# A two-layer graph attention network in f32: the second layer's aggregates 1 to 4 split a second time

## The chip, the cores and the metric

The kernel runs on one core of one Trainium2 chip. The metric is the device time of one execution in microseconds (us). The engines are called PE (TensorE, the matrix unit; PEld is its loading of weights), DVE (VectorE), ACT (ScalarE), POOL (GpSimd) and SP (SyncE, which here only issues transfers).

## The reference, cut to what matters

N is 2708 nodes, all widths are 1024, everything is float32. Each layer normalises its rows, makes attention weights under the mask `adj`, and multiplies them by rows:

```python
h = jnp.maximum(_layernorm(x, axis=-1), 0.0)
# layer 0
f, g = h @ Wf + bf, h @ Wg + bg
attention = softmax(jnp.where(adj > 0, relu(f @ g.T), -9e15), axis=1)
x = x + attention @ (h @ W + bW)
# layer 1 (on the new x and its own h)
hw = h @ W
e = leaky_relu(hw @ a1 + (hw @ a2).T, 0.2)
attention = softmax(jnp.where(adj > 0, e, -9e15), axis=1)
x = x + relu(attention @ hw)
```

## The kernel before

**Order of products.** Attention times (h times W) is computed as (attention times h) times W. The first product is called the aggregate, the second the projection. Every big product is done by a form of Strassen's scheme with seven products of halves in place of eight, here named M1 to M7. Each needs sums of the operands' quarters, and sums of the results.

**Tiles.** The 2708 rows are twenty tiles of 128 rows, a tile MONO of 128 and a tile TINY of 20. The output is made in five panels `p`, of 576, 576, 532, 512 and 512 rows (`width`). The twenty tiles form ten pairs (`pairs`, NQ = 10); a panel owns two pairs, 2p and 2p + 1.

**Stages.** Layer 0 goes panel by panel: scores, the next panel's `project_q`, `aggregate(0, p)`, `project(0, p)`. As a panel's projection ends, its rows of x are complete; `rows_done` normalises them and `pair_h` forms, for a pair of tiles, the seven first-level combinations of rows and stores them in DRAM, in `hg_d[1]`, one tensor for two pairs, in rows of 512 elements. Layer 1 then runs, for each panel, `aggregate(1, p)` and `project(1, p)` (lines 1544 to 1550).

**An aggregate** (line 841). The left operand is a tile of row combinations from DRAM (`hc`, 128 x 2 x 512, loaded on SP), the right one is a weight tile `S[t]` (128 x width) or a first-level sum of weight tiles' halves. `accumulate` (line 603) walks through the products in the order M1, M5, M2, M6, M3, M7, M4; each is 10 pairs x 4 column groups `d`, a matmul of 128 x 128 by 128 x h with h half the panel's width (line 617), into four PSUM banks, one for each `d`. An evict function per product adds the bank to what is kept in SBUF. The sums of the weights are made on DVE: `T1` at the start, `second` after M5, `fourth` after M2 (10, 20 and 10 subtractions of 128 x h). `left_over` (line 877) adds MONO's and TINY's part. After M3, `inverse_sums` inverts the row sums of the weights; after M7, `scale` (line 931) multiplies the results by them on POOL.

**What orders the work.** Loads keep the order in which the program issues them. Other instructions are put in order for each engine by a planner at build time. Small steps of DVE and ACT work wait in a list, `later`. Each step has an estimated cost; `behind(us)` (line 198) adds credit after a group of matmuls and issues steps from the list while credit is left. A step's own loads are issued up to `ahead` steps earlier. `exps_until` forces the weights' steps when they are needed.

**The next panel's weights.** `take_shifts(p + 1)` (line 1536) empties the list and makes the row maxima; `take_weights(p + 1)` (line 1540) puts 24 steps at the front of the list, 22 of which load a mask and do two ACT and up to three DVE operations on a weight tile. In layer 1 they hang on the products M3 and M7, the fifth and sixth in order (line 1548).

**Buffers.** `slots` holds 54 buffers of 128 x 576 (weights, temporaries), `strm` 12 buffers of 128 x 1024 (everything loaded in a stream, `hc` too), `psum` 8 banks.

## Time and profile before

| | us |
|---|---|
| median of three runs | 3134.34 (3131.34 to 3138.29) |
| span of the profiled execution | 3135.8 |
| layer 1, aggregate 0 (2157.3 to 2309.2) | 151.9 |
| layer 1, aggregate 1 (2357.1 to 2507.4) | 150.3 |
| layer 1, aggregate 2 (2569.1 to 2707.6) | 138.5 |
| layer 1, aggregate 3 (2760.3 to 2893.8) | 133.5 |
| layer 1, aggregate 4 (2941.7 to 3073.9) | 132.2 |

The profiled execution's own run time is not given apart; its span, from the first instruction to the last, lies 1.5 us above the median of the runs. All stage times are read from the span's start. The mean granted clock of TensorE is 0.989. In a group of instructions the first number is busy time, then the mean length of one in ns, then the engine's idle time before them and what ended it. A single matmul's length includes the time until its last result is out, so lengths of neighbours overlap; the time between starts is what a stream of them costs.

### The profile page before, as it was taken

What the parts mean: (1) busy time and instruction counts of PE and PEld (TensorE: products, weight loads), DVE (VectorE), ACT (ScalarE), POOL (GpSimd) and SP (SyncE); (2) the same over time, 40 slices, a digit from 0 to 9 for tenths busy, and PEclk for the clock granted to TensorE, in tenths of its full rate; (3) what the DMA queues carried; (4) which work ended last, traced back from release to release, by engine and by line L of the source; (5) the groups of instructions that cost most, each with busy time, mean ns of one, the idle gap of its engine ahead of it and who ended that gap; (6) DMA issues with size and microseconds to landing.
All of it is one profiled execution on the core that took longest, in us unless ns stands there. A gap on an engine that the chain in (4) does not pass through costs nothing.

```text
span 3135.8 us, 36310 instructions
## 1 busy us (share of the span) xinstructions
PE 3053.1 (97%) x12694; PEld 2266.1 (72%) x12694; DVE 1835.6 (59%) x3767; ACT 450.3 (14%) x785; POOL 427.3 (14%) x654
## 2 busy tenths in 40 slices
PE   8998999899999999999999999998999999999998
PEld 4576777657877588886888885875757758678684
DVE  5766693776741686426973377758573571745612
ACT  3420020010200101101020002103131130311200
POOL 1421101310002110023000101021010020120202
PEclk9999999999999999999999999998999999999999
DMA  6989967988546796468955678597655565565655
GB/s 220 294 252 248 292 247 253 301 275 230 175 136 156 222 247 223 149 153 253 284 180 160 171 214 245 191 293 250 200 179 175 158 200 158 171 197 172 219 169 181
DMA packets 386278, 666.04 MB, mean 212 GB/s; under 512 B 171744, under 2 KB 212224, under 8 KB 386096
## 3 DMA queue, kind: packets, MB, share of 16 engines
q1 hardware_dynamic: 341936, 536.96, 56.9%
q0 software_dynamic: 44160, 126.76, 12.6%
q8 instruction: 101, 1.65, 0.2%
q14 instruction: 81, 0.66, 0.1%
HBM read 548.26 MB, written 115.30 MB: 212 GB/s over the span
## 4 chain that ended last, share of the span: by engine, by line
PE 81%; issue 6%; DVE 6%; DMA 5%; SPq 1%; POOL 1%; ACT 0%; POOLq 0%; DVEq 0%; ACTq 0%
PE gz L617 11%; PE gx L617 11%; PE gy L617 10%; PE sz L1140 6%; PE pz L1029 5%; PE gv L617 5%; PE sx L1140 4%; PE sy L1140 4%; PE px L1029 4%; PE py L1029 4%; PE M_ps L530 3%; PE qz L617 2%; PE qx L617 2%; PE qy L617 2%; DVE junk L45 1%
## 5 line engine op out<-in xcount | busy, mean ns | idle before, releaser
L1140 PE MATMUL sz<-B,As 128*128 128x288 f32 (+2 forms) x1200 | 295.9, 396 | 12.1 <-DVE st L45 7.9
L1140 PEld LDWEIGHTS sz<-B,As 128*128 128x128 f32 x1200 | 229.4, 192 | 63.1 <-DVE st L45 11.8
L933 POOL TENSOR_TENSOR gT<-gT,rr 128x2304 f32<-128x2304 f32 (+5 forms) x20 | 73.0, 3648 | 1081.4 <-DVE rr L45 979.3
L1140 PE MATMUL sx<-B,As 128*128 128x288 f32 (+2 forms) x800 | 201.5, 395 | 11.2 <-DMA As<-hs_d 9.1
L1140 PE MATMUL sy<-B,As 128*128 128x288 f32 (+2 forms) x800 | 199.3, 392 | 0.0
L617 PE MATMUL gz<-Sa,hc 128*128 128x288 f32 (+2 forms) x800 | 190.3, 399 | 5.9 <-DMA hc<-hg_d 5.9
L617 PE MATMUL gx<-P,hc 128*128 128x288 f32 (+2 forms) x800 | 187.0, 394 | 0.1
L617 PE MATMUL gz<-P,hc 128*128 128x288 f32 (+2 forms) x800 | 185.5, 392 | 0.0
L1140 PEld LDWEIGHTS sx<-B,As 128*128 128x128 f32 x800 | 152.5, 191 | 45.2 <-DMA As<-hs_d 10.1
L617 PE MATMUL gy<-T,hc 128*128 128x288 f32 (+2 forms) x800 | 184.2, 391 | 0.0
L617 PEld LDWEIGHTS gz<-Sa,hc 128*128 128x128 f32 x800 | 154.6, 194 | 40.0 <-DMA hc<-hg_d 6.4
L617 PEld LDWEIGHTS gx<-P,hc 128*128 128x128 f32 x800 | 152.4, 191 | 34.2 <-issue 3.7
L1140 PEld LDWEIGHTS sy<-B,As 128*128 128x128 f32 x800 | 152.3, 191 | 30.8
L617 PEld LDWEIGHTS gz<-P,hc 128*128 128x128 f32 x800 | 151.3, 190 | 31.6 <-issue 1.8
L617 PEld LDWEIGHTS gy<-T,hc 128*128 128x128 f32 x800 | 152.0, 190 | 30.5
L1029 PE MATMUL pz<-w,ps 128*128 128x512 f32 x320 | 142.1, 594 | 0.8 <-DVE pt L45 0.8
L1029 PE MATMUL py<-w,ps 128*128 128x512 f32 x320 | 141.9, 593 | 0.0
L1029 PE MATMUL px<-w,gT 128*128 128x512 f32 x320 | 141.0, 593 | 0.0
L143 POOL DMA_DIRECT2D out_dram<-x_res x180 | 89.2, 502 | 269.7 <-DVE x_res L45 264.5
L1029 PEld LDWEIGHTS pz<-w,ps 128*128 128x128 f32 x320 | 60.2, 190 | 77.1 <-issue 71.0
L1029 PEld LDWEIGHTS py<-w,ps 128*128 128x128 f32 x320 | 60.6, 190 | 75.5 <-issue 73.1
L530 PE MATMUL M_ps<-wgT,wfT 128*128 128x512 f32 x256 | 112.9, 597 | 1.6 <-ACT hsT L45 1.6
(319 smaller groups left out, 4894.9 us busy)
## 6 DMA issues: line engine op xcount, KB each, us to landing
hc<-hg_d SPq DMA_DIRECT2D x350, 512.0 KB, 3.7
As<-hs_d SPq DMA_DIRECT2D x150, 512.0 KB, 5.2
w<-wt_d SPq DMA_DIRECT2D x96, 512.0 KB, 4.9
w<-in_L_gnn_W_dram SPq DMA_DIRECT2D x72, 512.0 KB, 4.8
md<-md_d SPq DMA_DIRECT2D x56, 512.0 KB, 5.7
adj_i<-in_adj_dram SPq DMA_DIRECT2D x200, 128.0 KB, 5.2
hs_d<-hsT POOLq DMA_DIRECT2D x40, 512.0 KB, 7.2
As<-hs_d SPq DMA_DIRECT2D x50, 256.0 KB, 4.8
```

The source lines that it names most:

```text
L45: i = f(*a, **k)
L143: nc.gpsimd.dma_start(a, b)
L530: nc.tensor.matmul(ps, wfT[a][c // NH][:, c % NH, :], wgT[b][c], start=(c == 0), stop=(c == NC - 1))
L617: nc.tensor.matmul(ps[d], left(m, k, d), right(m, k), start=(start and k == 0), stop=(k == K - 1), skip_group_check=True)
L933: nc.gpsimd.tensor_tensor(of(e, s), of(e, s), by(s, k), OP.mult)
L1029: nc.tensor.matmul(ps, left[i][m][:, k, :], w_[k], start=(start and k == 0), stop=(k == NH - 1), skip_group_check=True)
L1140: nc.tensor.matmul(ps[:n, :h], lefts[q][:, i % 2, c, :n], B[m][c // 2][:, c % 2, :h], start=(start and c == 0), stop=(c == NH - 1), skip_g ...
```

## The change

Aggregates 1 to 4 of layer 1 apply the seven-product scheme a second time, inside each of the seven products. Aggregate 0 of layer 1 and all of layer 0 keep one level.

- **Rows.** `hg_d[1]` is replaced by one tensor `hr_d`, whose rows lie in halves of 256 elements, and a tensor `hs2_d` holds the four second-level combinations that aren't rows of `hr_d` themselves. `put_quarters` makes them: for each product and each two pairs, two fetches on POOL's queue, four DVE operations of 128 x 256, two stores. These 35 steps wait in a second list, `lazy`, from which `behind` issues only when `later` is empty and `spare` is set: in layer 0's aggregates 1 to 4 and in layer 1's aggregate 0. What is still open when a product needs it is forced by `quarters_until`.
- **Aggregate.** `aggregate_quartered` runs the seven outer products in the order M1, M5, M2, M6, M7, M3, M4. Each is seven inner products of 5 x 2 matmuls of 128 x 128 by 128 x (h/2), both column groups in one bank. The inner M4 of an outer product follows the first inner product of the next one. Their results are joined in SBUF (`V`) and added to the places in G by `into_place`. `quarters_of` makes the second-level sums of the weights, 20 subtractions for each outer product, in the middle of the outer product before. `scale` runs in the last outer product.
- **Loads.** Each inner product loads 128 x 4 x 256; the fifth of the five row groups comes from two tiles loaded once for each outer product. Aggregate 0 of layer 1 reads its rows from `hr_d` in pieces of 256.
- **Next weights.** `take_shifts` hangs on M2 and `take_weights` on M6, the third and fourth outer product, except in aggregate 0, which keeps M3 and M7. The first outer product's sums are made in the projection before, at M7.

The diff, cut to its core:

```diff
-    hg_d = [[dram.tile([P, 7, len(g), W], FP, name=f"hg{l}_d{i}") for i, g in enumerate(groups)] for l in range(2)]
+    hg_d = [dram.tile([P, 7, len(g), W], FP, name=f"hg_d{i}") for i, g in enumerate(groups)]
+    NK = NQ // 2
+    WH = W // 2
+    hr_d = dram.tile([P, 7, 2, 2, NK, WH], FP, name="hr_d")
+    hs2_d = dram.tile([P, 7, 4, NK, WH], FP, name="hs2_d")
...
+        while spare[0] and not later and lazy and credit[0] > 0:
+            credit[0] -= one(lazy)
...
+    def put_quarters(m, k):
+
+        two = []
+
+        def fetch():
+            if from_slots[0]:
+                two.extend(slot(f"hq{h}", (P, 2, WH)) for h in range(2))
+            else:
+                t = stream("hq", (P, 4, WH))
+                two.extend(t[:, 2 * h:2 * h + 2] for h in range(2))
+            for h in range(2):
+                nc.gpsimd.dma_start(two[h], hr_d[:, m, h, :, k])
+
+        def go():
+            a11, a12, a21, a22 = (two[h][:, i] for h in range(2) for i in range(2))
+            add(a22, a21, a22)
+            sub(a21, a11, a21)
+            sub(a11, a22, a11)
+            sub(a12, a12, a11)
+            for h in range(2):
+                store(hs2_d[:, m, 2 * h:2 * h + 2, k], two[h])
+            made_quarters[m] = made_quarters.get(m, 0) + 1
+        put(1.7, go, fetch, to=lazy)
...
+        def make(m):
+            for k in range(NK):
+                r11, r12, r21, r22 = (part_of(m, k, i) for i in ((0, 0), (0, 1), (1, 0), (1, 1)))
+                four = slot("quarter", (P, 4, WX // 4))
+                t = {n: four[:, i, :hb] for i, n in enumerate((M5, M6, M7, M4))}
+                sub(t[M5], r12, r11)
+                sub(t[M6], r22, t[M5])
+                sub(t[M7], r22, r12)
+                sub(t[M4], r21, t[M6])
+                sums[m, k] = t
...
+        def product(m, n, ps, start):
+            quarters_until(m)
+            if (m, 0) not in lasts:
+                for i, of in enumerate((hr_d[:, m, :, :, NK - 1].rearrange("p h f c -> p (h f) c"), hs2_d[:, m, :, NK - 1])):
+                    lasts[m, i] = stream("hl2", (P, 4, WH))
+                    load(lasts[m, i], of)
+            t = stream("hc2", (P, NK - 1, WH))
+            raw = n in (M1, M2, M4)
+            i = {M1: 0, M2: 1, M4: 3, M6: 0, M3: 1, M7: 2, M5: 3}[n]
+            load(t, hr_d[:, m, i // 2, i % 2, :NK - 1] if raw else hs2_d[:, m, i, :NK - 1])
+            last = lasts[m, int(not raw)][:, i]
+            for k in range(NK):
+                for d in range(2):
+                    lhs = t[:, k] if k < NK - 1 else last
+                    nc.tensor.matmul(ps[:, d], lhs[:, d * P:(d + 1) * P], inner_right(m, n, k),
+                                     start=(start and k == 0 and d == 0), stop=(k == NK - 1), skip_group_check=True)
+            behind(fine)
...
+        def into_place(m, V, r):
+            for e, s in place[m]:
+                o = quad(e, s)[:, 2 * r:2 * r + 2]
+                if m == M1:
+                    nc.scalar.copy(o, V[r])
+                elif m == M5:
+                    add(o, o, quad(0, lo)[:, 2 * r:2 * r + 2])
+                else:
+                    add(o, V[r], o)
...
+        before_next = {M1: lambda: make(M5), M5: with_second, M2: lambda: (of_right["fourth"](), make(M6)), M6: lambda: make(M7),
+                       M7: lambda: make(M3), M3: lambda: make(M4)}
...
+            X = bank2("gx")
+            product(m, M1, X, True)
+            nc.scalar.copy(c21, X)
+            if m == M1:
+                of_right["fifth"]()
+            if left_out:
+                left_out()
+            Z = bank2("gz")
+            product(m, M6, Z, True)
+            add(c12, Z, c21)
+            Y = bank2("gy")
+            product(m, M5, Y, True)
+            add(c22, Y, c21)
+            if m == M7:
+                corner()
+            if m in before_next:
+                before_next[m]()
+            product(m, M2, X, False)
+            if m not in more_of:
+                nc.scalar.copy(c11, X)
+            product(m, M7, Z, False)
+            add(c22, Z, c22)
+            product(m, M3, Y, False)
...
+            add(c12, Y, c12)
...
-            then = {M3: lambda p=p: take_shifts(p + 1), M7: lambda p=p: take_weights(p + 1)}
-        g = aggregate(1, p, S, sm, then, rate=4.0)
-        project(1, p, g, finish1(p), by_pair=(p == NP - 1), rate=1.7)
+            then = dict(zip((M2, M6) if p else (M3, M7), (lambda p=p: take_shifts(p + 1), lambda p=p: take_weights(p + 1))))
+        spare[0] = p == 0
+        g = aggregate_quartered(p, S, sm, next_right, then, fine=1.0) if p else aggregate(1, p, S, sm, then, rate=4.0)
+        hooks = {}
+        if p + 1 < NP:
+            next_right = quarters_of(p + 1, got["P"][0])
+            hooks = {M7: next_right["first"]}
+        project(1, p, g, finish1(p), hooks, by_pair=(p == NP - 1), rate=1.7)
```

## The prediction

> **What bounds the kernel now.** I read the page's busy times first, then the busy times by stage of the second layer (windows cut where TensorE goes from aggregates to projections), then the groups by shape, then the order in time.
>
> ```profile
> PE 3053.1 (97%) x12694; PEld 2266.1 (72%) x12694; DVE 1835.6 (59%) x3767; ACT 450.3 (14%) x785; POOL 427.3 (14%) x654
> ```
> ```profile
> 2357.10:2507.40 150.30, 150.30 (x645) 115.83 (x644) 63.74 (x123) 20.98 (x38) 11.60 (x10) 1.00 0.53 162
> 2507.40:2569.10 61.70, 61.70 (x146) 27.26 (x145) 40.81 (x62) 20.33 (x33) 14.12 (x29) 1.00 0.55 171
> ...
> 2760.30:2893.80 133.50, 133.50 (x642) 115.54 (x641) 57.43 (x118) 18.98 (x34) 10.81 (x10) 1.00 0.59 180
> 2893.80:2941.70 47.90, 47.90 (x113) 21.11 (x113) 38.10 (x59) 17.19 (x28) 11.85 (x24) 1.00 0.69 209
> 2941.70:3073.90 132.20, 132.20 (x630) 114.34 (x629) 34.59 (x80) 6.73 (x14) 10.79 (x10) 1.00 0.59 183
> ```
>
> These stages are, in order, panel 1's aggregate and projection, panel 3's two, and panel 4's aggregate. The columns are length, then PE, PEld, DVE, ACT, POOL, clock, DMA share, GB/s. PE is busy for every microsecond: the aggregates of layer two are TensorE time and nothing else. So time falls only if TensorE gets less to stream and is still fed.
>
> Next, how long a matmul takes. Each matmul of the source is two instructions (a product has 10 x 4 matmuls, and 80 stand in a row):
>
> ```profile
> 2357.23 19.40 PE gx L617 x80
> ```
> ```profile
> 2760.31 17.43 PE L617 MATMUL gx<-P,hc 128*128 128x256 f32 x80
> ```
> ```profile
> 61.64 1.04 PE L238 MATMUL sp_ps<-ident,v 128*128 128x128 f32 x8
> 62.52 1.91 PE L399 MATMUL h_ps<-ident,x 128*128 128x128 f32 x16
> ```
> ```profile
> 62.41 1.78 PEld L399 LDWEIGHTS h_ps<-ident,x 128*128 128x128 f32 x16
> 64.16 0.30 PEld L530 LDWEIGHTS M_ps<-wgT,wfT 128*128 128x128 f32 x2
> ```
>
> At 288 columns: 19.40 / 80 = 0.2425 us. At 256 columns: (17.43 - 0.38 for the last one's drain) / 79 = 0.2158. At 128 columns, with new weights each time, the 16 transposes take (1.91 - 0.27) / 15 = 0.1091. All three lie on one line, 0.834 ns per column and almost nothing fixed, so a matmul of half the width costs half.
>
> **What the Trainium skill says.** "TensorE: Matmul & The Clock Gate", LDWEIGHTS (loading the stationary operand): a load takes the number of columns over 1.2 GHz, 107 ns for 128. Groups by shape record an ordinary f32 load here as 190 ns, which would swamp a 128-column matmul. But the two ordinary loads in the row at 64.16 together last 0.30 = 0.11 + 0.19: the second started 0.11 after the first. So 190 is latency, the engine is held about 0.11 us, and the page fits. "VectorE: DVE Perf Modes", the errata section on SBUF-source operations: a fixed cost per instruction, whatever the size. It agrees: subtractions run 0.367 us apart at 288 elements and 0.335 at 256 (rows below), about 0.07 of it fixed. "GPSIMD Engine Reference", Specifications: its SBUF interfaces are shared with VectorE where a VectorE instruction has two SBUF inputs. It agrees, and strikingly:
>
> ```profile
> 2464.36 5.05 POOL L933 TENSOR_TENSOR gT<-gT,rr 128x2304 f32<-128x2304 f32 x1 [98.87 <-DVE rr L45]
> ```
> ```profile
> 2465.14 4.30 DVE L45 TENSOR_TENSOR z<-f,mcol 128x5 f32<-128x5 f32 x1
> ```
>
> A five-column operation lasted 4.30 us, until POOL's scaling ended. "DMA: Bandwidth & Descriptors", Specifications: line rate from 512 bytes on, so I cost the new 1 KB pieces of the sums' rows at their bytes; no row here isolates such a load.
>
> **The change part by part.** *Aggregates 1 to 4, matmuls.* Before: 7 x 10 x 4 x 2 = 560 instructions of h = 288, 266, 256, 256 columns. After: 49 x 5 x 2 x 2 = 980 of 144, 133, 128, 128. By the line: 560 x (0.2425, 0.2242, 0.2158, 0.2158) = 135.8, 125.6, 120.8, 120.8. After, 980 x (0.1224, 0.1133, 0.1091, 0.1091) = 120.0, 111.0, 106.9, 106.9. It saves 15.8 + 14.6 + 13.9 + 13.9 = **58.2 us**, all on the path. The left-over rows keep their work (16 instructions of h become 32 of h/2 over twice the banks, and the short ones go in groups of four as before): 0.
>
> *Second-level sums of the weights.* 7 x 5 x 4 = 140 subtractions of 128 x h/2 per panel on DVE.
>
> ```profile
> 2363.16 3.03 DVE L45 TENSOR_TENSOR T<-P 128x288 f32<-128x288 f32 x8
> ```
> ```profile
> 2764.51 3.10 DVE L45 TENSOR_TENSOR T<-P 128x256 f32<-128x256 f32 x9
> ```
>
> (3.03 - 0.45) / 7 = 0.367 and (3.10 - 0.42) / 8 = 0.335, hence about 0.216 at 144, 0.20 at 128: 30 us for panel 1, 28 for 3 and 4. *Evictions:* 38 + 4 of h elements for 28 before, 14 x 0.335 to 0.367 = 5. *Placing into G:* 16 of 2h elements, at twice 0.335 less the fixed 0.07, so 0.6 to 0.67: 10. The old 40 sums stay. So DVE gains 46 us in panel 1 and 42 in panel 3. The ledger of aggregate plus projection: panel 1, 63.7 + 40.8 + 46 = 150 of 212 - 16 = 196 us (77%); panel 3, 57.4 + 38.1 + 42 = 138 of 181 - 14 = 167 (82%); panel 4, which makes no next weights, near half. It fits, but no longer loosely. An inner product is now 20 instructions, 2.2 to 2.4 us, and a bank is wanted again two products later, so DVE may be late by some 4.4 us; a block of sums is 20 x 0.2 = 4, with a first-level block ahead of it 7 to 11. Behind such a block queue the evictions, and behind these TensorE. And the scaling's two POOL operations (5.1 + 2.6 us) now fall in the last outer product, beside the next weights' two-input additions, which they lock out. I put the waits at 4 us in panels 1 to 3 and 2 in panel 4: **+14**. Bounds: 0 (it all fits into the slack), and 4 x 29 = 115 (no sum is hidden).
>
> *Next weights earlier (third and fourth outer product).* The same instructions; 24 items at credit 2.1 against 21 inner products at 1.0 and the projection's 14 x 1.7, so about 10 in the aggregate, 11 in the projection, 3 in the next aggregate. The mask loads pass some aggregate loads on SP; these are fetched ahead. I cost the move at 0: the products M7, M3 and M4 and the projection hide it. If that cover is gone, every item that is late (three DVE operations, 2 us) stands ahead of the next aggregate's sums; with three left, 6 us a panel.
>
> *Loads of aggregates 1 to 4.* 35 of 512 KB become 49 + 14, +14.7 MB. Panel 3 moved 24.09 MB in its window, and the end of layer one shows what the engines can do:
>
> ```profile
> DMA packets 9782, 24.09 MB, mean 180 GB/s; under 512 B 1167, under 2 KB 3215, under 8 KB 9774
> ```
> ```profile
> DMA packets 9468, 24.23 MB, mean 362 GB/s; under 512 B 1076, under 2 KB 2612, under 8 KB 9465
> ```
>
> 38.8 MB in 133.5 - 14 = 119.5 us is 325 GB/s: below 362, with eight or nine tiles of 2.2 us fetched ahead. Taken as hidden; bounds 0 and, at the 301 GB/s of the busiest slice of the page, 129 - 119.5 = 9.5 us a panel.
>
> *Second-level sums of the rows.* 35 items of four DVE operations of 256 elements (1.34 us, 47 in all), two fetches and two stores each on POOL's queue, at 0.5 to 1.0 us an issue by POOL's groups. They lie in aggregates of layer one whose DVE is busy 36 to 39 us of 132 to 148 (82 of 132 in the last), and in aggregate 0 of layer two (106 of 152). POOL's queue waits there for fetched data; behind it stand mask stores and the scaling, none wanted within microseconds. Their 36.7 MB add 7.3 MB a stage. Only the end of layer one is open, where TensorE waits 8.3 and 3.9 us on a chain that began with mask loads 13.6 us long: **+4** for this, for the 1 KB pieces in aggregate 0 and for the split stores. Bounds: -1 (order shifts that chain either way) and 15.
>
> **Sum.** 58.2 - 14 - 4 = 40 us saved. The profiled span is 3135.8, 1.5 above the median of the runs, 3134.3, so it is a typical execution, and what lies around it doesn't change: 3134.3 - 40 = **3094**.
>
> **The rivals.** *Everything fits:* 3134 - 58 = 3076; the ledger of 77 to 82% speaks for it, the 4.4 us of tolerance against. *The transfers bind:* all four panels pay 9.5, and 3134 - 40 + 38 = 3132, no change; for it speaks 325 GB/s wanted, against it 362 held for 67 us. *The slower one: VectorE's blocks come between.* If each of the 28 outer products waits for its sums, the point from which it decides is 58.2 / 28 = 2.1 us each; at 2.8 us, two thirds of a block, they cost 78 us, and it ends at 3154. For it: first-level and second-level blocks stand together ahead of M2 and M6. Against: sums are issued half an outer product (7 to 9 us) early. *The weight load binds:* if 190 ns held the engine, 980 x 0.19 x 4 = 745 against 503 us before, 3376; the pair at 64.16 speaks against it. That the change doesn't do what it says I can't see: no condition but the panel's number chooses the split.
>
> **How the numbers follow.** Forecast (3076 to 3114) 0.60; everything fits 0.07; more is eaten but still faster (3114 to 3128) 0.08; transfers bind 0.08; VectorE's blocks 0.14; weight load 0.03. A measurement of this kernel tells 0.2%, 6 us, from no change, so faster is 0.75, the same 0.08, slower 0.17. The range 3074 to 3136 leaves out the last two and half of the second.
>
> **What would show it.** Right: narrow matmuls 0.109 to 0.123 us apart; aggregates of 135 to 139, 124 to 128, 120 to 124 and 118 to 120 us; DVE near 80% there; single TensorE gaps of 1 to 3 us released by DVE. Wrong: 0.19 spacing; gaps released by the row tiles' loads; gaps of over 2 us at every outer product; a longer stretch between the two layers.

## The result, and the profile after

| | before | after |
|---|---|---|
| median of four runs each, us | 3136.32 (3131.34 to 3140.34) | 3127.83 (3126.43 to 3136.15) |
| span of the profiled execution, us | 3135.8 | 3127.1 |

The ratio of the times is 0.9978, 95% interval 0.9958 to 0.9999. A repeat on another chip (21 runs of the changed kernel, 43 of the one before) gave 0.9989, 0.9982 to 0.9995. So by the two ratios the change saves 7 and 3 us where 40 were forecast; it lies at the edge of what a measurement tells from no change. Layer one and layer two are here what the code calls layers 0 and 1.

The page's busy times after the change:

```profile
PE 3016.9 (96%) x14630; PEld 2311.3 (74%) x14630; DVE 2068.1 (66%) x4587; ACT 463.0 (15%) x817; POOL 536.3 (17%) x794
```

The busy times by stage: panel 1's aggregate and projection, panel 3's two, panel 4's aggregate, then the last projection of layer one; under it the same projection before the change. The columns are length, PE, PEld, DVE, ACT, POOL, clock, DMA share, GB/s:

```profile
2364.40:2517.80 153.40, 142.01 (x1129) 138.11 (x1128) 111.17 (x293) 25.75 (x49) 12.95 (x12) 0.96 0.76 250
2517.80:2579.60 61.80, 61.80 (x147) 27.36 (x146) 42.44 (x75) 19.35 (x31) 14.09 (x29) 1.00 0.61 193
...
2766.10:2897.00 130.90, 126.11 (x1125) 123.97 (x1124) 101.29 (x275) 22.89 (x43) 11.91 (x11) 0.97 0.86 292
2897.00:2945.10 48.10, 48.10 (x115) 21.31 (x114) 39.73 (x72) 17.21 (x28) 11.79 (x24) 1.00 0.75 234
2945.10:3067.40 122.30, 121.15 (x1114) 119.89 (x1113) 73.70 (x229) 8.71 (x20) 11.08 (x10) 1.00 0.90 305
2086.30:2164.40 78.10, 57.56 (x133) 25.36 (x131) 48.33 (x121) 10.70 (x19) 22.38 (x31) 0.87 1.02 341
```
```profile
2090.00:2157.30 67.30, 54.26 (x136) 24.85 (x134) 48.67 (x122) 10.77 (x19) 12.84 (x23) 0.89 0.98 360
```

Before, PE was busy for the whole of each aggregate, at clock 1.00. Now 11.4 of 153.4 us and 4.8 of 130.9 are idle, and the clock in the same stages is 0.96 and 0.97. Panel 4, where DVE has least to do (73.7 of 122.3 us), gained most, 9.7 us; panel 1 lost 3.1.

Where the time went, by the starts of the stages in both traces (aggregates 1 to 4 are those of layer two):

| stage, us | before | after |
|---|---|---|
| up to the first aggregate of layer one | 451.7 | 445.4 |
| last aggregate of layer one | 132.1 | 134.0 |
| last projection of layer one | 67.0 | 78.1 |
| aggregate 1 | 150.2 | 153.3 |
| aggregate 2 | 138.4 | 133.6 |
| aggregate 3 | 133.3 | 130.9 |
| aggregate 4 | 132.0 | 122.3 |

The four aggregates give 13.8 us, the end of layer one takes 13.1 back. The 6.3 us in the first row are chance: the edit doesn't touch that stretch, and in the seventeen further profiled executions, all with it unchanged, it ended anywhere from 438.9 to 452.1, and on one chip alone from 440.8 to 452.1.

The narrow matmuls themselves run as forecast. TensorE in order of time, at the start of aggregate 4 (start, length, then the group):

```profile
2945.09 1.95 PE L1066 MATMUL gx<-P,hc 128*128 128x128 f32 x16
2946.88 0.61 PE L1066 MATMUL gx<-P,hl 128*128 128x128 f32 x4
```

(2946.88 - 2945.09) / 16 = 0.112 us apart, half of the 0.2158 of before and a little over. The same view in aggregate 1, around its longest wait:

```profile
2364.45 2.12 PE L1066 MATMUL gx<-P,hc 128*128 128x144 f32 x16
...
2371.31 0.65 PE L1066 MATMUL gy<-quarter,hl 128*128 128x144 f32 x4
2377.29 4.21 PE L1066 MATMUL gx<-P,hc 128*128 128x144 f32 x16 [5.33 <-ACT gT L45]
2381.29 1.17 PE L1066 MATMUL gx<-P,hl 128*128 128x144 f32 x4
2383.77 2.23 PE L1066 MATMUL gz<-quarter,hc 128*128 128x144 f32 x16 [1.30 <-DVE gT L45]
```

Sixteen matmuls take 2.12 us, but 4.21 after the wait of 5.33, and the four after them 1.17 instead of 0.65. So a wait costs twice: the gap, and then a stretch at half speed. The clock in the trace says the same: it is 0.50 for 6.83 us at each of the four longest waits of the aggregates (from 2375.85, 2488.49, 2686.47 and 2870.78). What is left of these stretches when TensorE starts again holds 23.6 us of matmuls, 20 to 38 at a time, so half of it, 11.8 us, is lost. The wait of 1.30 that follows here leaves the speed alone (2.23).

What TensorE waited for in aggregates 1, 3 and 4, waits under 1 us left out (us in total, times, longest):

```profile
PE gx L1066 <- ACT gT L45: 5.3, 1, 5.3
PE gz L1081 <- DVE V L45: 3.9, 2, 3.3
PE gz L1066 <- DVE gT L45: 1.3, 1, 1.3
```
```profile
PE gz L1081 <- DVE V L45: 3.3, 1, 3.3
PE gz L1066 <- DVE gT L45: 1.1, 1, 1.1
```
```profile
PE gz L1066 <- DVE gT L45: 1.2, 1, 1.2
```

None is for a row tile: with the transfers at 0.90 of their time in aggregate 4 they still don't bind. The 3.3 us wait is the same place in aggregates 1, 2 and 3: the left-over rows of the sixth outer product want a bank that DVE has not yet emptied. DVE in order of time just before it, in aggregate 1:

```profile
2486.57 0.71 DVE L45 TENSOR_TENSOR sm<-sm,P 128x532 f32<-128x532 f32 x1 [0.71 <-ACT P L45]
2487.20 0.77 DVE L45 SCALAR_TENSOR_TENSOR P<-ub,f,P 128x532 f32<-128x532 f32 x1
2488.01 0.71 DVE L45 TENSOR_TENSOR P<-P,maskl 128x532 f32<-128x532 f32 x1
2488.64 0.45 DVE L45 TENSOR_TENSOR V<-gz,V 128x288 f32<-128x288 f32 x1
```

The 0.45 us addition that TensorE needs (V<-gz) stands behind items of the next panel's weights, one of which waits for ScalarE. Nothing needs these items soon.

The other two kinds of wait have another neighbour each. ScalarE just before the 5.3 us wait in aggregate 1, and DVE just before the 1.2 us wait in aggregate 4:

```profile
2376.27 0.68 ACT L45 ACTIVATE P<-P 128x576 f32<-128x576 f32 x1 [2.35 <-DVE P L45]
2376.86 0.38 ACT L45 COPY gT<-gx 128x288 f32<-128x288 f32 x1
```
```profile
2951.86 3.09 DVE L45 TENSOR_TENSOR T<-P 128x256 f32<-128x256 f32 x9
2954.88 0.40 DVE L45 TENSOR_TENSOR gT<-gz,gT 128x256 f32<-128x256 f32 x1
```

The copy of the first X (gT<-gx) stands behind an exponential of the late weights, which waits for DVE. The addition in aggregate 4 stands behind a block of first-level sums; each of the four aggregates has such a wait near its start, of 1.15 to 1.40 us, 5.0 us in all.

### The profile page after: what moved, and what is told of

It reads as the page before. It is cut to its first block, busy times and chain, and to the rows that moved or that the text cites. A ratio compares the mean times of both kernels' runs of the same rounds, so it can differ in the third digit from the quotient of the medians.

```text
span 3127.1 us, 41677 instructions
## 1 busy us (share of the span) xinstructions
PE 3016.9 (96%) x14630; PEld 2311.3 (74%) x14630; DVE 2068.1 (66%) x4587; ACT 463.0 (15%) x817; POOL 536.3 (17%) x794
## 4 chain that ended last, share of the span: by engine, by line
PE 70%; DVE 13%; DMA 7%; issue 7%; SPq 1%; POOL 1%; ACT 1%; POOLq 0%; DVEq 0%; ACTq 0%
PE sz L1377 6%; PE gx L661 6%; PE gy L661 6%; PE gz L661 5%; PE gz L1066 4%; PE sx L1377 4%; PE sy L1377 4%; PE pz L1266 4%; PE px L1266 4%; PE py L1266 3%; PE M_ps L574 3%; PE gy L1066 3%; PE gx L1066 2%; PE gv L661 2%; DVE P L45 2%
## 5 line engine op out<-in xcount | busy, mean ns | idle before, releaser
L1377 PEld LDWEIGHTS sz<-B,As 128*128 128x128 f32 x1200 | 228.7, 191 | 58.2 <-DVE st L45 12.0
L1377 PEld LDWEIGHTS sx<-B,As 128*128 128x128 f32 x800 | 153.6, 193 | 47.2 <-DMA As<-hs_d 7.0
L661 PEld LDWEIGHTS gz<-Sa,hc 128*128 128x128 f32 x800 | 153.6, 193 | 39.3 <-DMA hc<-hg_d 6.1
L1377 PEld LDWEIGHTS sy<-B,As 128*128 128x128 f32 x800 | 152.3, 191 | 32.5 <-ACT x L45 1.9
L1066 PE MATMUL gz<-quarter,hc 128*128 128x128 f32 (+2 forms) x1344 | 169.4, 279 | 6.5 <-DVE gT L45 5.0
L1066 PEld LDWEIGHTS gz<-quarter,hc 128*128 128x128 f32 x1344 | 160.6, 191 | 9.0 <-DVE gT L45 6.5
L1266 PE MATMUL px<-w,gT 128*128 128x512 f32 x320 | 141.0, 593 | 0.0
L143 POOL DMA_DIRECT2D mk_d<-mask x55 | 35.8, 650 | 532.5 <-DVE mask L45 526.4
L1266 PEld LDWEIGHTS px<-w,gT 128*128 128x128 f32 x320 | 60.2, 190 | 71.1 <-issue 69.3
L661 PE MATMUL gy<-T,hc 128*128 128x288 f32 (+2 forms) x480 | 111.6, 394 | 0.0
L977 POOL TENSOR_TENSOR gT<-gT,rr 128x2304 f32<-128x2304 f32 (+5 forms) x12 | 44.4, 3698 | 357.9 <-DVE rr L45 164.3
L661 PEld LDWEIGHTS gy<-T,hc 128*128 128x128 f32 x480 | 91.2, 190 | 19.5
```

What stands on the lines that cost most here:

```text
L143: nc.gpsimd.dma_start(a, b)
L661: nc.tensor.matmul(ps[d], left(m, k, d), right(m, k), start=(start and k == 0), stop=(k == K - 1), skip_group_check=True)
L977: nc.gpsimd.tensor_tensor(of(e, s), of(e, s), by(s, k), OP.mult)
L1066: nc.tensor.matmul(ps[:, d], lhs[:, d * P:(d + 1) * P], inner_right(m, n, k), start=(start and k == 0 and d == 0), stop=(k == NK - 1), ski ...
L1266: nc.tensor.matmul(ps, left[i][m][:, k, :], w_[k], start=(start and k == 0), stop=(k == NH - 1), skip_group_check=True)
L1377: nc.tensor.matmul(ps[:n, :h], lefts[q][:, i % 2, c, :n], B[m][c // 2][:, c % 2, :h], start=(start and c == 0), stop=(c == NH - 1), skip_g ...
```

## The experiments

**Two theories at first.** A: the work on DVE is too much; the second-level sums come between. B: the amount fits, but its order in the queues (DVE's, and those that issue transfers) puts work that nobody waits for ahead of work that TensorE waits for. The stage lengths below are from one profiled execution each; the ratios are to the kernel before on the same chip, whose median there was 3127 to 3136 us. Times of different chips are therefore compared by ratio.

| kernel | last aggregate, last projection of layer one | layer two: aggregate 0 | aggregates 1, 2, 3, 4 | ratio (95%) |
|---|---|---|---|---|
| before | 132.1, 67.0 | 151.7 | 150.2, 138.4, 133.3, 132.0 | 1 |
| after | 134.0, 78.1 | 151.9 | 153.3, 133.6, 130.9, 122.3 | 0.9978 (0.9958 to 0.9999) |
| after, repeat | 136.2, 75.8 | 153.0 | 154.4, 133.6, 130.9, 122.3 | 0.9989 (0.9982 to 0.9995) |
| e1 row sums not at the end | 132.1, 67.0 | 177.2 | 154.3, 133.5, 130.9, 122.3 | 1.0034 (1.0021 to 1.0048) |
| e2 scaling on DVE | 133.5, 78.5 | 152.1 | 152.3, 133.9, 128.1, 122.3 | 0.9976 (0.9966 to 0.9985) |
| e3 no sums of weights | 133.8, 77.8 | 152.2 | 145.0, 124.4, 122.5, 120.8 | 0.9918 (0.9903 to 0.9932) |
| e4 program order | 136.4, 76.2 | 152.8 | 145.0, 131.7, 127.4, 123.6 | 0.9960 (0.9945 to 0.9975) |
| e5 next weights late | 132.7, 80.2 | 152.8 | 146.2, 133.6, 131.2, 130.1 | 0.9984 (0.9978 to 0.9991) |
| e6 fetches on SP | 132.1, 78.4 | 152.0 | 153.3, 133.8, 130.9, 122.3 | 0.9993 (0.9984 to 1.0001) |
| e7 = e1 and e6 | 132.1, 66.9 | 162.6 | 154.3, 133.6, 130.9, 122.3 | 0.9985 (0.9975 to 0.9995) |
| e8 = e2, e4, e6 | 132.1, 80.2 | 152.0 | 141.7, 127.5, 125.1, 122.3 | 0.9922 (0.9910 to 0.9934) |
| e11 fetches on ScalarE | 132.1, 77.5 | 152.2 | 153.4, 133.7, 131.0, 122.3 | 0.9986 (0.9978 to 0.9995) |
| e12 = e2, e4 in aggregates 1 to 3, e11, and panel 1's weights early | 132.1, 78.9 | 153.8 | 135.9, 127.5, 125.1, 122.3 | 0.9893 (0.9880 to 0.9906) |
| e14 buffers from the streamed tiles | 132.1, 92.0 | 153.0 | 153.4, 133.9, 130.9, 122.2 | one execution |
| e14b = e14 and e11 | 132.1, 84.7 | 155.4 | 152.0, 133.8, 131.0, 122.3 | one execution |
| e15 = e12 and e14 | 132.1, 86.3 | 154.0 | 135.8, 127.5, 125.1, 122.3 | 0.9927 (0.9908 to 0.9945) |
| e16 = e12 and e1 | 132.1, 67.0 | 160.5 | 135.9, 127.5, 125.1, 122.2 | 0.9891 (0.9873 to 0.9910) |
| e17 = e16, fetches on SP | 132.1, 66.9 | 165.8 | 135.9, 127.5, 125.1, 122.3 | 0.9909 (0.9893 to 0.9926) |

**The repeat.**

> The changed kernel as it is, a second time, on the chip of the runs that follow, so that they can be compared with it and not only with the kernel before. Ratio to the kernel before 0.998 (0.996 to 1.000), and each stage of layer two within 1 us of the first profile: aggregates 1 to 4 at 153.3, 133.6, 130.9 and 122.3 us, last projection of layer one 78.1 us, aggregate before it 134.0 us. What is open: the stretch up to the first scores, which the edit does not touch, was 387.9 us in the profile before and 381.7 after. If that was chance, a repeat gives any value between them; if the edit reached it in some way, it gives 381 to 383 again.

The aggregates of layer two lie within 1.1 us of the first profile. The end of layer one takes 212.0 us in place of 212.1, but divided otherwise: its aggregate 2.2 us longer, its projection 2.4 us shorter, outside the 1 us expected. The first stretch ended at 440.8: chance. A difference of 1 us in one stage, or of 2 in one of these two, says nothing by itself.

### The amount of work and its order on DVE

**e3, the second-level sums of the weights left out.** `make` does nothing, and `right` hands out unsummed quarters:

```diff
-            return sums[m, k][n] if n in sums[m, k] else part_of(m, k, {M1: (0, 0), M2: (1, 0), M3: (1, 1)}[n])
+            return part_of(m, k, {M1: (0, 0), M2: (1, 0), M3: (1, 1), M5: (0, 1), M6: (1, 1), M7: (0, 1), M4: (1, 0)}[n])
```

> Leaves out the 140 second-level subtractions of the weights in each of the panels 1 to 4; the matmuls that took these sums take raw quarters of the same size, so TensorE's work is the same and the result is not the product. Theory 'amount of DVE work': nearly all waits on DVE and ACT in the aggregates go (22.7 us in the four) and with them the half-speed stretches (about 14), and the aggregates fall to about 133, 123, 120 and 119 us. Rival 'lock' or 'planner's order': waits of 3 us at M3's left-over rows stay in panels 1 to 3.

The four aggregates fall by 27.3 us (540.1 to 512.8). Aggregates 2, 3 and 4 have no wait left at all, aggregate 1 still has 6.5 us of them. Both theories allow that: with fewer operations, fewer also stand in front of others.

**e4, DVE in program order.** The planner may not reorder DVE inside `aggregate_quartered`:

```diff
+        nc.hold = ("vector",)
         inverse = []
...
         nc.vector.tensor_tensor(o, o, by(lo, NH, h), OP.mult)
+        nc.hold = ()
```

> All work as in the changed kernel, but in the aggregates 1 to 4 DVE's instructions keep the order of the program, so that the planner doesn't place evictions. Theory 'planner's order': the additions that empty the banks then come earlier than the next weights' steps that are behind them in the program, and the waits shrink by half or more (aggregates 5 us shorter in panels 1 to 3). Rival 'amount': same waits within 3 us, or longer, since blocks of sums now stand whole in front of evictions.

12.4 us less (540.1 to 527.7) with the same operations: 8.3, 1.9 and 3.5 in aggregates 1 to 3, where about 5 each were expected, and 1.3 more in aggregate 4. That is order, not amount; aggregate 2 alone wouldn't tell them apart.

**e2, the scaling on DVE in place of POOL.**

```diff
-                nc.gpsimd.tensor_tensor(t, t, by(s, NH, k), OP.mult)
+                nc.vector.tensor_tensor(t, t, by(s, NH, k), OP.mult)
```

> In aggregates 1 to 4 the scaling by the inverse sums runs on DVE and not on POOL (about 4 us more DVE work for each panel, no locking out of DVE's two-input operations, which cost 3.1 us and 5.4 us in panel 1's trace). Theory 'lock': the waits of 3.3 us at the left-over rows of the sixth outer product (M3) come from the lock; they vanish in panels 1 to 3 with the half-speed stretch after them, and the aggregates 1 to 3 shrink by 5 to 7 us each. Rival 'amount of DVE work': the waits stay or grow, and the aggregates are within 2 us of 153, 134 and 131.

-1.0, +0.3, -2.8 and 0.0 us, where 5 to 7 less were expected in each of the first three. The waits at the left-over rows of the sixth outer product don't vanish: they are 4.6, 4.4 and 2.8 us in aggregates 1 to 3, where they were 3.3. So these waits can't be put down to the lock-out of DVE by POOL's scaling, to which the prediction gave a share. Moving the scaling brings some 3.5 us net, of which only the 2.8 in aggregate 3 are clear of the 1.1 us by which a stage differed in the repeat; the ratio isn't told apart from the changed kernel's.

**e5, the third part of the change undone.**

```diff
-            then = dict(zip((M2, M6) if p else (M3, M7), ...
+            then = dict(zip((M7, M3) if p else (M3, M7), ...
```

> Undoes the third part of the change alone: in panels 1 to 3 the shifts and weights of the next panel are begun after the fifth and sixth outer product, as before the change, not after the third and fourth. Theory (the early start is needed, since VectorE has little room beside the halves): the work that is left over runs into the next aggregate, as in aggregate 1, whose weights still start that late; aggregates 2, 3 and 4 grow by 3 to 9 us each, by a wait for the copy of the first X, while aggregates 1 to 3 lose 0 to 3 us of waits: the whole 5 to 20 us over the changed kernel. Rival (the early start does harm, since its items stand ahead of additions that TensorE waits for): aggregates 1 to 3 lose the 3.3 to 3.9 us waits of the left-over rows and what follows them, 3 to 6 us each, and the next ones don't grow: the whole 5 to 15 us under it.

Aggregate 1 gets 7.1 us shorter, 2 and 3 stay, 4 gets 7.8 longer: 541.1 against 540.1. Both theories of the expectation are half right. TensorE's waits in aggregates 3 and 4 of this run, those under 1 us left out:

```profile
PE gx L1066 <- ACT gT L45: 5.1, 1, 5.1
```
```profile
PE gx L1066 <- ACT gT L45: 6.1, 1, 6.1
```

The 3.3 us wait is gone, since no weight item stands there any more, and every aggregate now begins with the wait that only aggregate 1 had: ScalarE's copy of the first X queued behind an exponential, which waited for DVE to get to the late weights. So the early start moves a wait rather than removing one; by itself it is worth nothing that can be measured here.

**e8, three edits together** (e2, e4 in aggregates 1 to 3, e6):

> Three edits together: VectorE's instructions in program order in aggregates 1 to 3 (aggregate 4, where that order cost 1.3 us, stays with the planner), the scaling on VectorE, the row sums' fetches on SP. If the parts are independent: aggregate 1 at 143 to 146 us, aggregate 2 at 131 to 132, aggregate 3 at 125 to 128, aggregate 4 at 122, last projection of layer one at 68 to 78; together 12 to 24 us under the changed kernel, so a ratio to the kernel before of 0.990 to 0.994. Rival: in program order the scaling stands in VectorE's queue ahead of additions that TensorE waits for, and takes back its gain: aggregates 1 to 3 as with program order alone (145.0, 131.7, 127.4) or 1 to 3 us above.

Aggregates 1 to 3 fall by 11.6, 6.1 and 5.8 us (153.3, 133.6, 130.9 to 141.7, 127.5, 125.1), more than e2 and e4 added up (9.3, 1.6, 6.3) in two of the three. One wait over 2 us is left, at the beginning of aggregate 1 (4.0, for the copy of X). The last projection of layer one is not among the gains: 80.2 us, where 68 to 78 were expected.

**e12, and panel 1's weights one outer product earlier**, so that they don't run over into aggregate 1, with the row sums' fetches on ScalarE's queue:

```diff
-            then = dict(zip((M2, M6) if p else (M3, M7), ...
+            then = dict(zip((M2, M6) if p else (M6, M3), ...
```

> Program order on VectorE in aggregates 1 to 3, scaling on VectorE, row sums' fetches on ScalarE's queue, and panel 1's weights begun one outer product earlier in aggregate 0 of layer two (shifts after the fourth, weights after the fifth). If the parts add up: aggregates 1 to 4 as with the three parts together (141.7, 127.5, 125.1, 122.3), of which aggregate 1 loses its 4.0 us wait for the first X and the slow matmuls after it (137 to 139), and the last projection of layer one is 66 to 71 us: the whole 7 to 16 us under the combination before, so 3091 to 3101 us where that had 3107.5. Rival: the earlier weights lengthen aggregate 0 (152.0 us) by as much as aggregate 1 gains, because the row sums' rest and the shifts then meet on VectorE.

Aggregate 1 is 135.9 us. The only wait in it, and the stage's row in the busy times:

```profile
PE gz L1081 <- DVE V L45: 0.7, 1, 0.7
```
```profile
2363.20:2499.10 135.90, 135.23 (x1129) 133.03 (x1128) 105.84 (x272) 23.14 (x44) 3.91 (x8) 1.00 0.84 278
```

DVE is busy 105.8 us of a stage that is 17.4 shorter than in the changed kernel, and the clock is back at 1.00. Some 10.4 us of waits went (11.1 to 0.7), and 7 more with them, 5.7 of these by the half-speed matmuls. Over the four aggregates 29.3 us went (540.1 to 510.8): the idle time fell from 22.6 to 5.9 and the half-speed loss from 11.8 to 0, together 28.5. The last projection of layer one stays at 78.9 us, where 66 to 71 were expected.

**Theory A is left with little.** The four aggregates take no more than with the sums left out (512.8), with all the sums and the scaling on DVE. But aggregates 2 to 4 of e3 are still 3.1, 2.6 and 1.5 us shorter, 7.2 in all, which the sums still cost there. The greater part of the loss was what stood ahead of what: the order on DVE, the scaling's place and the late start of panel 1's weights together, of which order alone gave 12.4 (e4).

### The end of layer one

**e1, no row sums in the last aggregate of layer one**; its seven steps (fourteen fetches, fourteen stores) fall into aggregate 0 of layer two, which then has fourteen steps.

```diff
-        spare[0], from_slots[0] = p > 0, p == NP - 1
+        spare[0], from_slots[0] = 0 < p < NP - 1, p == NP - 1
```

> The seven row-sum steps that lay in layer 0's last aggregate run in layer 1's aggregate 0 instead; nothing else differs. Theory 'queue': at the end of layer 0 their fetches and stores stand on POOL's queue ahead of the additions of the bias to x_res, which then land late in a full DMA system, so that DVE can't empty the projection's banks and TensorE waits 6.1 us and goes on at half speed. Then the last projection of layer 0 shrinks from 78.1 back to about 67 us, the last aggregate of layer 0 from 134.0 to about 132, and the whole by 11 to 13 us, to about 3115. Rival 'bytes': the split stores and the pieces of 1 KB slow the same stretch; then it stays within 3 us of 78.

The end of layer one is back to the length it had before (132.1 and 67.0), so the row sums are the cause of all 13.1 us. The 11 to 13 us expected for the whole don't come: aggregate 0 of layer two pays 25.3, nearly all in one wait:

```profile
PE sum_ps L864 <- DVE gT L45: 23.4, 1, 23.4
```

Each fetch stands on POOL's queue behind stores that wait for DVE, and DVE, in order, waits 4.8 to 5.9 us for each of four pairs of fetches, with the evictions behind it.

**e6, the fetches on SP's queue**, and **e11, on ScalarE's**:

```diff
-                nc.gpsimd.dma_start(two[h], hr_d[:, m, h, :, k])
+                load(two[h], hr_d[:, m, h, :, k])
```

> The row sums' fetches go to SP's queue in place of POOL's; nothing else is changed. Theory of the queue: the bias transfers of the last projection of layer one stood behind fetches and stores of the row sums on POOL's queue, and each such transfer takes POOL about 0.7 us to issue; with half of them gone from that queue the last projection falls from 78.1 to 68 to 74 us and the aggregate before it stays at 133 to 134 us, 4 to 10 us in all. Rival, the stores alone do it, since they are what waits for VectorE: 76 to 79 us, no gain. Rival, the fetches now stand ahead of the weights' tiles on SP's queue and these come late: 80 us or more.

> The row sums' fetches go to ScalarE's queue, the third one; nothing else is changed. On POOL's queue they stood ahead of the bias transfers (6.1 us of waiting), on SP's they stood ahead of the weight tiles (9.2 us). Theory of the queues: ScalarE has nothing to do in that stretch that TensorE needs within microseconds, so the last projection of layer one falls from 78.1 us (75.8 in the repeat) to 66 to 71, with 132 to 134 us for the aggregate before it: 7 to 14 us under the changed kernel. Rival (VectorE's sums themselves, 28 of 0.42 us, come in the way wherever their input is fetched): 74 to 79 us. Rival against: a fetch that waits for its place holds up ScalarE's copies, and the aggregates of layer one grow by 1 us or more each.

The projection stays at 78.4 and 77.5 us; the theory of the queue fails as I had put it. What it says of POOL's queue is true. The bias transfers of that stretch, in the changed kernel and in e6 (KB each, median us from issue to landing):

```profile
x_res<-in_L_gnn_bW_dram POOLq DMA_DIRECT2D x8, 256.0 KB, 16.9
```
```profile
x_res<-in_L_gnn_bW_dram POOLq DMA_DIRECT2D x8, 256.0 KB, 5.8
```

But a second cause was waiting right behind. TensorE's waits in the last projection, in the changed kernel and in e6:

```profile
PE mx_ps L849 <- DVE mx L45: 8.3, 1, 8.3
PE pz L1266 <- DVE pt L45: 6.1, 1, 6.1
PE sp_ps L253 <- DVE m L45: 3.9, 1, 3.9
```
```profile
PE px L1266 <- DMA w<-in_L_gnn_W_dram: 9.2, 1, 9.2
PE mx_ps L849 <- DVE mx L45: 8.3, 1, 8.3
PE sp_ps L253 <- DVE m L45: 3.9, 1, 3.9
PE pz L1266 <- DVE pt L45: 0.8, 1, 0.8
```

(8.3, 3.9 and 0.8 were there before the change as well.) The wait for the bias has become one for weight tiles: in e6 the second rival's mechanism, though not its 80 us or more. SP's queue in e11, where the fetches aren't on it, and in e7, where no row sums fall in this stretch:

```profile
2058.23 13.29 SPq L139 DMA_DIRECT2D x_res<-in_x_dram  x8
...
2087.97 0.90 SPq L139 DMA_DIRECT2D w<-in_L_gnn_W_dram  x2
```
```profile
2062.65 4.88 SPq L139 DMA_DIRECT2D x_res<-in_x_dram  x8
...
2085.34 0.94 SPq L139 DMA_DIRECT2D w<-in_L_gnn_W_dram  x2
```

In e11 the first loads of residual rows take 13.3 us to issue and in e7 4.9; the weight tiles come 8.5 us after the start of the projection (2079.5), in e7 3.1 us before it (2088.4). What SP waited for in e11, from 2030 on, and in e14b below (us in total, times, longest):

```profile
SPq L139 <- DMA hq<-hr_d: 17.4, 7, 3.6
```
```profile
SPq L139 <- DMA hs_d<-hq: 22.1, 4, 12.8
```

In e11 these are the landings of the row sums' fetches, which SP's loads don't read. A wait for a buffer would end with the row sums' stores (hs_d<-hq), as in e14b; so the theory that the residual rows wait for the row sums' buffers, on which e14 and e14b were built, has nothing in e11's trace for it. The trace's semaphores show another way: the transfers of SP's and ScalarE's queues share eight semaphores that tell of landings, and each new transfer waits until the one that had its semaphore before has landed. A fetch moved to ScalarE's queue therefore still stands in SP's way; one on POOL's doesn't in this way. The weight tiles stand behind all this. The landings themselves were slow: over the 30 us that end 10 us before the projection, the DMA share was 1.02 in e11 and 0.76 in e7. Whether the full DMA engines alone would have made the tiles late, no run tells.

**e14, the row sums' buffers from the other pool**, that of the streamed tiles, fetches on POOL; **e14b**, the same with the fetches on ScalarE's queue; **e15**, as e14b, in e12. One execution each for the first two.

```diff
-        spare[0], from_slots[0] = p > 0, p == NP - 1
+        spare[0], from_slots[0] = p > 0, False
```

> The row sums of the last aggregate of layer one take their tiles from the pool of the streamed tiles and not from that of the residual rows; their fetches stay on POOL's queue. If the bias transfers are late because of POOL's queue, the last projection stays at 76 to 79 us with a 6 us wait for the bias sum. If the residual rows' loads wait for places that the row sums hold, and the weight tiles behind them on SP's queue with them, it falls only with the next run, where the queue is free as well. If the streamed tiles now lack places, the aggregate before it grows from 132 to 134 us to 136 or more.

> As the run before, with the fetches on ScalarE's queue. With the fetches on that queue and the tiles from the shared pool, SP's queue spent 13.3 us on the first eight loads of residual rows (17.4 us waiting for the row sums' transfers) where it spends 4.9 without row sums, issued the next weight tiles 8.5 us after the projection had begun and not 3.1 us before it, and TensorE waited 7.9 us for them. Theory (two causes, the queue and the places, each enough alone): now neither is there, and the projection takes 66 to 70 us. Rival (VectorE's sums): 74 us or more, with waits for VectorE. Rival (the row sums' transfers hold the streamed tiles' places): 74 us or more, with waits for weight tiles.

> The best combination so far (program order on VectorE in aggregates 1 to 3, scaling on VectorE, fetches on ScalarE's queue, panel 1's weights one outer product earlier; 3098.89 us, ratio 0.9893) with the row sums' tiles of the last aggregate of layer one from the streamed tiles' pool. If the places were the rest of the loss at the end of layer one: 8 to 13 us less, 3086 to 3092 us, with aggregates 1 to 4 as there (135.9, 127.5, 125.1, 122.3). If not: 3095 to 3102 us.

The projection takes 92.0, 84.7 and 86.3 us: longer, and none of the three cases expected for e14. TensorE's longest wait for weight tiles is 13.9, 13.1 and 15.0 us. So the rival of e14b holds: in its trace SP waits 22.1 us for the stores of the row sums, whose buffers the streamed tiles want. e15 misses both of its ranges (3107.51 us). The seven steps stand in the way of the projection's loads in each of the five forms that ran (the changed kernel, e6, e11, e14, e14b): on POOL's or SP's queue, by the landings that SP waits for, or by their buffers. What of it could be avoided at this place is open.

**e7, e16: the row sums in aggregate 0 of layer two, fetches on SP's or ScalarE's queue.**

> Fetches of the row sums on SP's queue, and no row sums taken in the last aggregate of layer one (as in e1), so that the last fourteen steps fall into aggregate 0 of layer two. With fetches on POOL's queue that aggregate took 177.2 us in place of 151.9. If it was the order of that queue (a fetch behind stores that wait for VectorE, and VectorE in its turn waiting for the fetch), it is now 152 to 160 us, and with the last projection of layer one at 67 and the aggregate before it at 132 us the whole is about 10 to 13 us under the changed kernel. If it was the amount of work on VectorE, or the sums being needed by a fixed point, it stays at 170 us or more.

> The best combination so far (3098.89 us) with the last fourteen row sums taken in aggregate 0 of layer two, their fetches on ScalarE's queue. The last projection of layer one falls from 78.9 to 67 us. If the queue was all that made these sums dear in aggregate 0, that stage grows from 153.8 us to at most 157 and the whole ends at 3088 to 3092 us. If a fetch that waits for a place holds up the exponentials on ScalarE, aggregate 0 grows by 10 us or more and nothing is won: 3097 to 3110 us.

Aggregate 0 takes 162.6 us in e7 (one wait of 6.8 for a row tile behind a fetch) and 160.5 in e16; it was 177.2 with the fetches on POOL. That is just over the 152 to 160 that the order of the queue was to give in e7, and 6.7 us over e12 in e16, between its two cases: the queue was most of the cost, not all. e7 as a whole gains nothing (0.9985, beside 0.9978 and 0.9989 for the changed kernel), where 10 to 13 us were expected. Against e12, e16 wins 11.9 us at the end of layer one (211.0 to 199.1 for the two stages) and loses 6.7 in aggregate 0. A last kernel, e16 with the fetches on SP, was to tell whether SP does as well:

> The same with the fetches on SP's queue. Without the other parts aggregate 0 took 162.6 us there, with a 6.8 us wait for a row tile that stood behind a fetch. If that stays, about 3097 to 3100 us, no better than with the sums at the end of layer one; if the earlier weights leave less for VectorE to do late in aggregate 0, 3090 to 3096 us.

It doesn't: aggregate 0 took 165.8, with a wait of 9.2 us for a row tile, and the time was 3100.24 us. e12 and e16 are the fastest kernels found, 3098.89 and 3092.32 us on their chips, 1.1% under the kernel before; their intervals don't tell them apart.

### What sets the pace of the narrow matmuls

**e13: four of five column matmuls in aggregate 4 with 64 columns** (one execution; the result lacks the other half of these columns).

```diff
-                    nc.tensor.matmul(ps[:, d], lhs[:, d * P:(d + 1) * P], inner_right(m, n, k),
+                    some = slice(0, hb // 2) if p == NP - 1 and k else slice(0, hb)
+                    nc.tensor.matmul(ps[:, d, some], lhs[:, d * P:(d + 1) * P], inner_right(m, n, k)[:, some],
```

> Measures what sets the pace of the narrow matmuls: in aggregate 4 of layer two four of the five column matmuls of each product stream 64 columns in place of 128, with the same weight loads and the same transfers; the other half of these columns of the result is left out. If the pace of 112 ns at 128 columns is the stream (128 columns plus some ns), the 64-column ones stand 53 to 60 ns apart and the aggregate falls to 80 to 90 us, unless the row tiles come late. If it is the weight load, they stay at 105 to 112 ns and the aggregate at 117 to 122 us. If it is the transfers (0.90 busy in that stage), the spacing falls but waits for row tiles appear, and the aggregate ends near 110 us.

The stage grew from 122.3 to 156.3 us, which no theory had. TensorE in order of time, and the stage's busy times; the rows with hl have 64 columns only, those with hc twelve of sixteen:

```profile
2945.96 0.61 PE L1067 MATMUL gx<-P,hl 128*128 128x64 f32 x4
2946.41 1.95 PE L1067 MATMUL gz<-quarter,hc 128*128 128x128 f32 x16
...
2954.46 2.94 PE L1067 MATMUL gz<-quarter,hc 128*128 128x128 f32 x16 [1.19 <-DVE gT L45]
2957.20 1.06 PE L1067 MATMUL gz<-quarter,hl 128*128 128x64 f32 x4
2958.05 3.62 PE L1067 MATMUL gy<-P,hc 128*128 128x128 f32 x16
```
```profile
2944.20:3100.50 156.30, 155.11 (x1113) 153.66 (x1112) 73.83 (x229) 8.81 (x20) 11.08 (x10) 0.77 0.73 237
```

At first 64 columns take (2946.41 - 2945.96) / 4 = 0.112 us, exactly what 128 take: not the stream sets the pace but something that each matmul with new weights needs, as the theory of the weight load says. Then comes a wait of 1.19 us. In the changed kernel a wait of 1.15 at the same place cost nothing more (2.05 us for the next sixteen); here TensorE goes to half speed, (2958.05 - 2957.20) / 4 = 0.213, and the clock in the trace is 0.50 from 2955.3 for 71.7 us. Since the pace doubles with the halved clock, a fixed time for each instruction that doesn't follow this clock is excluded as well; that the load itself is what takes the 0.112 us is the reading that is left, not a measurement of it. Why the clock stayed down so long, this one execution doesn't show.

## Why the prediction was wrong, point by point

**The matmuls, 58.2 us: right, by 6 us too much.** The spacing is 0.123 and 0.113 us in panels 1 and 2, where 0.1224 and 0.1133 were forecast, but 0.112 where 0.1091 was, at 128 columns. On 980 instructions in two panels that is some 5.6 us. The line held at 144 and 133 columns; at 128 the spacing meets the weight load, 0.112 us by e13. The transposes that gave 0.1091 had a shorter load, which their row shows: 16 loads in 1.78 us, 0.109 apart, leave 0.14 for the last, where ordinary loads are recorded with 0.19. The rival of the weight load had the wrong duration (0.19) and the right idea.

**Waits for VectorE, +14: the step that failed.** The gaps alone are 11.4, 5.3, 4.8 and 1.15, so 22.6 us, and the half-speed matmuls after them lose another 11.8: 34.4 us in place of 14. The forecast named the blocks of sums as what would stand in front. They did, in the four waits of 1.15 to 1.40 us (5.0 in all), and these cost no speed. The costly waits it didn't name: items of the next weights ahead of one addition (3.3 us in three panels) and the copy of X on ScalarE behind late weights (5.3 in panel 1), both of them cases of order, as e4, e5, e8 and e12 show. "It fits, but no longer loosely" was true of the amount: 150 us of DVE work were forecast for panel 1's two stages and 153.6 measured, 138 and 141.0 for panel 3's. With order and late weights put right (e12) the four aggregates save 43.1 us (553.9 to 510.8). That is near the forecast's 58.2 - 14 = 44.2, but by luck: the waits there are 5.9 us, and the rest is the 5.6 that the matmuls fall short by and some 3.4 of left-over rows.

The second cost of a wait, the clock, was not in the sum at all. The Trainium skill has it ("TensorE: Matmul & The Clock Gate", the part on the HAM clock gate): the array's clock is halved after an idle window of about 3.4 us and restored after a busy one. The traces agree with the price (after 5.33 and 3.27 us of waiting the clock is 0.50, and a matmul takes 0.25 us for 0.1225) and with the length (the half-speed stretches of the aggregates last 3.41 or 6.83 us, e13 apart). They don't agree that a whole window must be idle. In aggregates 1 to 4 of the changed kernel, its repeat, e1 to e5, e8, e12, e13 and e16, every wait of 2.27 us or more had a half-speed stretch begin in it or after it. Of the shorter ones, up to 1.98 us, only two had one: the 1.19 us in e13, and 0.96 us in aggregate 2 of e4; the same 0.96 us at the same place in e12 and e16 had none. So what decides for short waits is open, and that the 64 columns were to blame in e13 isn't shown.

**Left-over rows, 0:** in e12, where nothing runs at half speed, they take 44.2 us in the four aggregates, from start to start and without waits, where they took 40.8 before: +3.4.

**Next weights earlier, 0: right in the number** (e5: 541.1 against 540.1), by luck: not because later products hide the move, but because it removes a wait of 5 to 6 us in aggregates 2 to 4 and puts one of 3.3 into 1 to 3.

**Loads, hidden: right.** 305 GB/s and a share of 0.90 in aggregate 4, and no wait for a row tile.

**The end of layer one and the rest, +4 (up to 15): 13.1, the second step that failed.** The text looked for what stood behind the fetches on POOL's queue in the aggregates and found "none wanted within microseconds". In the last aggregate the bias transfers of the coming projection are behind them, and these are wanted within microseconds; and what the steps' transfers do to the landings and the buffers that SP's loads wait for was not costed at all. Of the forecast's own signs of being wrong, the longer stretch between the two layers came true here (199.1 to 212.1 us).

**The rivals.** Transfers bind: the time (3132) is near, the mechanism is not there. VectorE's blocks come between: the mechanism's neighbour, at 0.8 us a product on average (22.6 / 28; 1.2 with the half speed), not the 2.1 from which it decides.

**The sum as measured:** 58.2 - 5.6 - 22.6 - 11.8 = 18.2, and the aggregates gave 13.8; the 4.4 us between are small spacings, most of them among the left-over rows. Less 13.1 at the end of layer one; and 6.3 of chance in that pair of executions, and another 2.5 after the last projection (13.5 to 11.0 us up to the end of the span), which no run took apart. What is left of the 8.7 us between the two spans, -0.8, are changes under 0.5 in single stages.

## What to carry to other kernels

When a change gives a second engine more work, adding up its busy time is not enough: look at what stands ahead, in that engine's order, of the few operations that the bounding engine waits for, and price each wait of some microseconds with the slow stretch after it. For work that is moved into another stage, list what is queued behind each of its transfers in that very stage, what must wait for them to land, and what takes buffers from the same pool; a second limit can lie right behind the first, so that undoing one alone shows nothing. Narrower matmuls pay only down to the width at which the weight load takes as long, here just over 128 columns (131, an estimate from the line of 0.834 ns a column and the 0.112 us).

## What the runs showed of the hardware that I had not expected

- With a new 128 x 128 f32 weight load for each, matmuls stand 0.112 us apart whether they stream 128 columns or 64 (e13), though the load is recorded with 0.19 us. At half clock it is 0.213 for both widths.
- Half speed came after every wait of 2.27 us or more, and the loss in matmuls (11.8 us) was half as much again on top of the gaps (22.6). Shorter waits seldom brought it: one of 1.19 us (e13), and of three equal ones of 0.96 us (e4, e12, e16) the first.
- Transfers issued from SP's and from ScalarE's queue waited for each other's landings (17.4 us in e11); those from POOL's queue had semaphores of their own.
- The stretch up to the first aggregate of layer one, the same in all these kernels, took 438.9 to 452.1 us: 13 us of chance, more than the effect of the change.
